# A meter of VectorE's backlog for the taps of a depthwise convolution, and tiles that rest behind their stores, in a four-layer vision kernel

## The chip, the core and the metric

The kernel runs on one core of a Trainium2 chip (trn2). The metric is the device time of one launch in microseconds; several runs are made and the median counts. The core has five engines with queues of their own, each worked off in order: PE (TensorE, with its weight loads listed as PEld), DVE (VectorE), ACT (ScalarE), POOL (GpSimd) and SP (SyncE, which here issues nearly all DMAs).

## The reference, cut to what matters

The input x has 4 images of 384 channels and 48 x 48 points, all float32. Four layers follow each other, each `x = x + layer(groupnorm(x))`:

```python
# layer 0: a state-space block over the 2304 points of an image, 768 inner channels, 16 states
xin, z = split(xs @ in_proj_w.T);  xin = silu(conv4(xin))
h = exp(dt * A) * h + dt * B * x;  y = sum(h * C)      # a scan along the points
out = layernorm((y + xin * D) * silu(z) @ out_proj_w.T)
# layer 1: 1x1 product, filter in 8x8 Fourier patches, depthwise 3x3, gate, 1x1 product
t = depthwise3x3(irfft2(rfft2(patches(x @ w_in)) * fft_filter));  out = (gelu(t1) * t2) @ w_out
# layer 2: depthwise 11x11 convolution with kernels made of 4 points
# layer 3: 4 experts, each relu(x @ w1 + b1) @ w2 + b2, weighted by a two-best gate
```

Layer 0 is the longest: per image 5 chunks of 460 or 464 points, 6 groups of 128 channels, 16 states, so 4 x 5 x 96 = 1920 scans of one tile each.

## The kernel before, in words

**One loop over the scans sets the order.** `scans` walks over u = 0 to 1919, and each u is a slot. A slot has one scan on DVE (L966), one decay `da` on ACT (L942), the product `bu` for three slots later on POOL (L953), and the product with C, which is done on DVE (L986) in a fast slot and on POOL (L995) in a slow one. From the second image on two slots of four are slow; in the first image it is one of three. PE adds up the states by transposing into PSUM (L886), three to five slots later. B and C are rows broadcast to 128 partitions by SP's DMAs (L930), issued three to four slots ahead into 3 and 4 buffers.

**Everything else is fitted in by tasks.** A task is a generator that yields before each step with a kind: "act" steps run at the start of a slot, "pe", "dve" and "pool" steps in the middle, "late" steps behind the slot's product. A step that yields n times before it is issued stands at least n slots later; `wait(n)` does only that. A lane holds a queue of tasks and runs up to `width` of them at a time. Lanes come in a fixed order: `aux` (layer 0's own work: projections L749 to L768, steps L866, gates L1023, out projections L1037 to L1050, norm and residual L1091 to L1095), `start` (work done early in the first image), `one` (layers 1 to 3 of the image before, up to the scores of the experts) and `two` (the experts of an image, whose first task needs the last task of lane `one`). Layers 1 to 3 of image b are queued in `one` at slot 480 (b + 1) + 42.

**Two things hold a step back.** `Meter(2.3, 3.7)` stands for PE's backlog in us: each slot takes 2.3 off and puts 0.44 on for the transposes, and a "pe" step with a weight waits until its weight fits under 3.7 (lane `aux` is let through but counted). A `Ring` stands for the buffers of a tag: a step that needs a buffer waits until the one that it would reuse is marked done. "Done" is said when the last reader is issued, so what it guards is the order of issue and not the end of a DMA.

**Layer 1** (L1306 to L1457): six strips of 8 rows an image. `patches` makes the Fourier filter in PSUM (the sum L1366 is DVE's); `finish_strip` runs the depthwise 3x3: nine taps on DVE for each of three channel groups (`taps`, L1413 the first, L1415 the others), one PSUM accumulator for all (`accr`), a copy or GELU on ACT between groups, two products (L1430, L1437), then three products on PE (L1443, L1447) with a sum and statistics on DVE (L1452, L1454), and a store (L1457). `slow_slot()` gives the taps 3 places in a slow slot and 2 in a fast one.

**Layer 2** (L1491 to L1582): bands of 9 or 10 rows; `load_band` brings the band into `xb` (L1513), `windows` runs 8 matmuls for a block of 8 rows (L1557), and the last adds the sum into `xb` (L1578, L1580) and stores it (L1582). `xb` has two buffers. **Layer 3**: scores (L1649 to L1671), then `experts`: for each of 4 experts 16 blocks of 144 points; `load3` brings x (`xe`, L1737) and from the second expert on the running sum y (`ye`, L1740), two products follow on PE (L1750), the sum on DVE (L1782, or three L1785 for the first expert) and a store (L1791) of y, or of x with the sum in it for the first expert, and of the output for the last. Behind the last scan the lanes are worked off, image 3 goes through layers 1 to 3, and `all_experts` does its experts from one set of weights (L1850 to L1882).

Of the kernel before, what the change touches and what calls it, by code (L numbers as in the profile page):

```python
# [16 lines left out]
P = 128  # L17
# [25 lines left out]

class Ring:


    def __init__(self, make, n):
        self.make, self.n, self.read = make, n, []

    def free(self, k=1):  # L50
        return all(self.read[: max(0, len(self.read) + k - self.n)])
# [6 lines left out]
    def done(self, k):  # L58
        self.read[k] = True


class Meter:


    def __init__(self, each, limit):
        self.each, self.limit, self.value = each, limit, 0.0

    def slot(self, given):
        self.value = max(0.0, self.value - self.each) + given
# [25 lines left out]
class Lane:  # L95
# [7 lines left out]
    def step(self, phase, slot, at=0):  # L103
        for task in self.active:
            if task.ended:
                continue
            kind, weight, ring, when = task.next
            if PHASE.get(kind, 1) != phase or task.after > slot:
                continue
            if weight and self.bound and self.meter.value + weight > self.meter.limit:  # L110
                continue
            if (ring and not ring[0].free(ring[1])) or (when and not when()):
                continue
            self.meter.value += weight
            task.move(slot)
        self.active = [t for t in self.active if not t.ended]
        while (
            self.queue and len(self.active) < self.width and self.queue[0].at <= max(at, slot)
            and all(t.ended for t in self.queue[0].needs)
        ):  # L120
            task = self.queue.pop(0)
            task.move()
            if not task.ended:
                self.active.append(task)

    def drain(self, slot, others=()):
        n = 0
        while self.queue or self.active:
            self.meter.value = 0.0
            for phase in range(3):  # L130
                for lane in (self, *others):
                    lane.step(phase, slot + n, 1 << 30)
            n += 1
            assert n < 20000, "stuck"
# [8 lines left out]
def tile_layers(ctx: ExitStack, tc: tile.TileContext, a: dict, out: bass.AP):  # L143
# [22 lines left out]
    gexp = const("gexp", [GROUPS, C], a["c_gexp"])  # L166
# [8 lines left out]
    def group_norm(st, bank, mean, rstd, name):  # L175

        mv = small.tile([P, CT, 2], F32, name=f"mv{name}", tag="mv")
        for ct in range(CT):
            nc.vector.bn_aggr(mv[:, ct, :], st[:, ct].rearrange("p k s -> p (k s)"))

        def to_groups(src, n, what):
            ps = bank(f"g{what}{name}")
            for ct in range(CT):
                nc.tensor.matmul(
                    ps[:GROUPS, :n], lhsT=gsel[:, ct, :], rhs=src(ct),
                    start=ct == 0, stop=ct == CT - 1,
                )
            return ps[:GROUPS, :n]

        def to_channels(src, n, what):  # L190
            ps = bank(f"c{what}{name}")
            for ct in range(CT):
                nc.tensor.matmul(
                    ps[:, n * ct : n * ct + n], lhsT=gexp[:, bass.ts(ct, P)], rhs=src,
                    start=True, stop=True,
                )
            return ps[:, : n * CT]

        grp = small.tile([GROUPS, 2], F32, name=f"grp{name}", tag="grp")
        nc.vector.tensor_copy(grp, to_groups(lambda ct: mv[:, ct, :], 2, "m"))  # L200
        nc.vector.tensor_copy(mean, to_channels(grp[:, 0:1], 1, "m"))
        dev = small.tile([P, CT], F32, name=f"dev{name}", tag="dev")
        nc.vector.tensor_sub(dev, mv[:, :, 0], mean)
        nc.vector.tensor_mul(dev, dev, dev)
        var = small.tile([GROUPS, 1], F32, name=f"var{name}", tag="var")
        nc.vector.scalar_tensor_tensor(
            var, to_groups(lambda ct: dev[:, ct : ct + 1], 1, "v"), GN_EPS, grp[:, 1:2],
            ALU.add, ALU.add,
        )
        nc.gpsimd.tensor_tensor(var, var, neghalf[:GROUPS, 0:1], ALU.pow)  # L210
        nc.vector.tensor_copy(rstd, to_channels(var, 1, "v"))

    def group_norm_steps(st, ring, mean, rstd, name):
# [15 lines left out]
        def to_channels(src, n, what):  # L229
            ps, k = ring.take(f"c{what}{name}")  # L230
            for ct in range(CT):
                nc.tensor.matmul(
                    ps[:, n * ct : n * ct + n], lhsT=gexp[:, bass.ts(ct, P)], rhs=src,
                    start=True, stop=True,
                )
            return ps[:, : n * CT], k
# [179 lines left out]
    with ExitStack() as first:  # L416
# [55 lines left out]
        stats0 = wp.tile([P, 2, CT, 2, 3, 6], F32, name="stats0")  # L472
# [86 lines left out]
        def scans(wk, mm, ring, meter, place, lanes, begin):  # L559
# [9 lines left out]
            def image_stats(b, ct, h):  # L569
# [4 lines left out]
                for k in range(3):  # L574
                    yield ("dve",)
                    nc.vector.bn_stats(stats0[:, b % 2, ct, h, k, :], t[:, bass.ts(k, LB)])

            def image_norm(b):
                yield from group_norm_steps(
                    stats0[:, b % 2].rearrange("p c h k s -> p c (h k) s"), ring,  # L580
# [4 lines left out]
            def early_stats(b, ct, h):  # L585
# [6 lines left out]
                for k3 in range(3):  # L592
                    yield ("dve",)
                    nc.vector.bn_stats(st[:, ct, h, k3, :], t[:, bass.ts(k3, LB)])
# [8 lines left out]
            def early_fold(b):  # L603
# [21 lines left out]
                yield ("dve",)  # L625
# [11 lines left out]
            def early_z(b, t, j):  # L637
# [22 lines left out]
                yield ("pool",)  # L660
# [28 lines left out]
            def fold(b, which):  # L689
# [22 lines left out]
                yield ("dve",)  # L712
# [25 lines left out]
            def project(i, j):  # L738
# [27 lines left out]
                yield ("dve",)  # L766
# [74 lines left out]
            def steps(i, p):  # L841
# [22 lines left out]
                yield ("dve",)  # L864
# [146 lines left out]
            def gate(i, m):  # L1011
# [9 lines left out]
                yield ("late",)  # L1021
# [4 lines left out]
            def out_proj(i, k):  # L1026
# [20 lines left out]
                yield ("dve",)  # L1047
# [4 lines left out]
            def layer_norm(i):  # L1052
# [8 lines left out]
                yield ("dve",)  # L1061
# [12 lines left out]
            def residual(i, ct):  # L1074
# [14 lines left out]
                yield ("dve",)  # L1089
# [86 lines left out]
            for tag, shape, n in (  # L1176
# [7 lines left out]
                    n,  # L1184
# [14 lines left out]
            with tc.manual_schedule():  # L1199
# [10 lines left out]
                for u in range(N + 6):  # L1210
# [17 lines left out]
                    meter.slot(0.44)  # L1228
                    soon = u % PAIR >= 8
# [25 lines left out]
                while aux.queue or aux.active:  # L1255
                    at += 1
                    meter.slot(0.0)
                    for phase in range(3):
# [5 lines left out]

        def slow_slot():
            return place[0] % 4 < 2

        def later(b, ring, accr):
# [11 lines left out]
            def slots(tag, shape, n):  # L1280

                return Ring(
                    lambda name: d["wk"].tile(shape, F32, name=name, tag=tag, bufs=n), n
# [11 lines left out]
            def begin1():  # L1295
# [3 lines left out]
                w = d["w_out"] = wk.tile([P, 2, C], F32, name=f"w_out1_{b}", tag="w_out", bufs=1)  # L1299
                nc.sync.dma_start(w[:, 0, :], a["L1_w_outT"][:P, :])  # L1300
                nc.sync.dma_start(w[64:P, 1, :], a["L1_w_outT"][P:, :])
# [38 lines left out]
            def patches(hb, wb):  # L1340
# [24 lines left out]
                yield ("late",)  # L1365
# [27 lines left out]
            def finish_strip(hb):  # L1393
# [7 lines left out]
                def taps(ct):  # L1401
# [3 lines left out]
                    room = 3 if slow_slot() else 2  # L1405
                    for k in range(9):
                        if not room:
                            yield ("dve",)
                            room = 3 if slow_slot() else 2
                        room -= 1  # L1410
# [18 lines left out]
                yield ("dve",)  # L1429
# [6 lines left out]
                yield ("dve",)  # L1436
# [3 lines left out]
                for ct in range(CT):  # L1440
# [3 lines left out]
                        ps[:, :LB], lhsT=w[:, 0, bass.ts(ct, P)], rhs=act[:, 0, :],  # L1444
# [3 lines left out]
                        ps[:, :LB], lhsT=w[64:P, 1, bass.ts(ct, P)], rhs=act[64:P, 1, :],  # L1448
                        start=False, stop=True,
                    )  # L1450
                    yield ("late",)
# [26 lines left out]
            xbs = slots("xb", [P, max(BANDS) * W], 2)  # L1478
# [68 lines left out]
            def windows(ct, k, r, first, last, final):  # L1547
# [26 lines left out]
                if last:  # L1574
                    yield ("late",)
# [5 lines left out]
                    yield ("pool",)  # L1581
# [40 lines left out]
            xg = slots("xg", [P, CT, LB], 2)  # L1622

            def begin3():
# [16 lines left out]
                yield ("dve",)  # L1641
# [4 lines left out]
            def scores_of(hb):  # L1646
# [23 lines left out]
                yield ("dve",)  # L1670
# [17 lines left out]
        def experts(b, ring, rings):  # L1688
# [15 lines left out]
            def begin(e):  # L1704
# [21 lines left out]
                yield ("late",)  # L1726
# [4 lines left out]
            def load3(s, e):  # L1731
                yield (
                    "pool", 0, None,
                    lambda: rings["xe"].free() and (not e or rings["ye"].free()),
                )
                x = take(("x", s, e), "xe", f"xe{b}_{s}_{e}")
                nc.sync.dma_start(x, strip(x3d[b], bass.ts(s, EB)))  # L1737
                if e:
                    y = take(("y", s, e), "ye", f"ye{b}_{s}_{e}")
                    nc.sync.dma_start(y, strip(y3d, bass.ts(s, EB)))  # L1740
                yield from wait(3)

            def block(s, e):
# [33 lines left out]
                yield ("late",)  # L1777
                key = ("y" if e else "x", s, e)
                x = d[key][0]
                if e:  # L1780
                    y = x.rearrange("p c t -> p (c t)")
                    nc.vector.tensor_add(y, ps[:, : CT * EB], y)  # L1782
                else:
                    for m in range(CT):
                        nc.vector.scalar_tensor_tensor(  # L1785
                            x[:, m, :], ps[:, bass.ts(m, EB)], b2_sum[:, m : m + 1],
                            x[:, m, :], ALU.add, ALU.add,
                        )
                ring.done(r)
                yield ("pool",)  # L1790
                nc.sync.dma_start(strip(out[b] if e == NE - 1 else y3d, bass.ts(s, EB)), x)  # L1791
                done(key)
# [106 lines left out]
        def of_experts(pool, sizes):  # L1899
            for tag, n in sizes.items():  # L1900
# [5 lines left out]
                    n,  # L1906
# [11 lines left out]
        meter = Meter(2.3, 3.7)  # L1918
        one, two = Lane(8, meter), Lane(4, meter)

        def begin(b):
# [10 lines left out]
            {"we": 1, "xe": 2, "ye": 2, "hr": 1},  # L1932
        )
        with (
# [7 lines left out]
            while not all(ring.read):  # L1942
# [6 lines left out]
        with (  # L1949
# [4 lines left out]
            of_experts(wk, {"we": 2, "xe": 3, "ye": 3, "hr": 3})  # L1954

            one.queue += later(NB - 1, ring, accr)
            while one.queue or one.active or two.queue or two.active:
                at += 1
                meter.slot(0.0)
                if not (one.queue or one.active):  # L1960
# [124 lines left out]
```

## Time and profile before

| | |
|---|---|
| median of 3 runs | 5400.23 us (5399.6 to 5402.55) |
| the profiled execution | 5405.14 us |
| its span, first to last instruction | 5403.1 us, mean granted TensorE clock 0.919 |
| busy: PE, PEld, DVE, ACT, POOL | 4646.1, 3666.7, 4067.1, 2989.0, 3363.1 us |
| first and last scan start | 86.5 and 4515.3 us |
| taps (L1415) | 576, 348.0 us in all, 615 ns each |
| SP's DMAs | 787.38 MB of 794.36 MB in all |

Busy times are sums over the whole span; stages with different limits lie in them, so the profile is read by stretches. A wait names the engine that stood, the line that it stood at, what released it, the total in us, how often, and the longest.

### The profile page before, as it was taken

Reading aid. Unit: us, or ns where it says so; the run is one execution under the profiler, and the core shown is the slowest. Engines: PE = TensorE matmul, PEld = TensorE weight load, DVE = VectorE, ACT = ScalarE, POOL = GpSimd, SP = SyncE. Lnnn points to the kernel's source line nnn. Section 1 sums busy time; section 2 is a strip of 40 time slices with the busy share of each in tenths; the row PEclk is TensorE's granted clock in tenths of the full one; section 3 lists DMA queues with packets and bytes.
Section 4 is the critical chain, followed back from the end, with each engine's and each line's share of the span. In section 5 each row is a group of like instructions: output and inputs, shape, how many; then the busy total and the mean of one; then the engine's idle time right before and its main releaser. Section 6 shows DMA issues by size and latency. Waiting matters only on the chain. (4 is left out here: it accounts for less than half of the span.)

```text
span 5403.1 us, 82006 instructions
## 1 busy us (share of the span) xinstructions
PE 4646.1 (86%) x27796; PEld 3666.7 (68%) x27796; DVE 4067.1 (75%) x5581; ACT 2989.0 (55%) x6632; POOL 3363.1 (62%) x3020
## 2 busy tenths in 40 slices
PE   5898877787768988888889988888799988999899
PEld 3555545454446766765668867665678877889799
DVE  5998899889997888889887778798987875452200
ACT  3566655565547765565567745565477653335321
POOL 3788778886677788876678678775677783000000
PEclk8898987788879999998899999998899999999899
DMA  4565545443344555655566565655566573543210
GB/s 152 172 187 175 178 128 150 129 143 120 111 127 131 148 165 157 191 161 147 149 172 178 161 200 155 173 146 149 154 182 174 158 213 115 175 138 105 64 27 23
DMA packets 648873, 794.36 MB, mean 147 GB/s; under 512 B 60149, under 2 KB 642661, under 8 KB 648062
## 3 DMA queue, kind: packets, MB, share of 16 engines
q1 hardware_dynamic: 638148, 787.38, 49.9%
q8 instruction: 221, 3.62, 0.3%
q10 hardware_dynamic: 10298, 1.67, 0.2%
q14 instruction: 206, 1.69, 0.1%
HBM read 685.04 MB, written 103.81 MB: 146 GB/s over the span
## 5 line engine op out<-in xcount | busy, mean ns | idle before, releaser
L953 POOL TENSOR_TENSOR bu<-u,B 128x460 f32<-128x460 f32 (+1 forms) x1920 | 2227.0, 1170 | 795.5 <-DVE g L966 349.8
L942 ACT ACTIVATE da<-dt,a_neg 128x460 f32<-128x460 f32 (+1 forms) x1920 | 1242.4, 648 | 310.6 <-DVE g L986 185.6
L886 PE MATMUL y<-ident,g 128*115 128x128 f32 (+1 forms) x7680 | 1111.3, 292 | 192.5 <-DVE g L986 114.8
L886 PEld LDWEIGHTS y<-ident,g 128*115 128x115 f32 (+1 forms) x7680 | 991.2, 183 | 400.4 <-DVE g L986 140.5
L995 POOL TENSOR_TENSOR g<-g,C 128x460 f32<-128x460 f32 (+1 forms) x885 | 1030.0, 1164 | 246.8 <-ACT carry L980 244.3
L966 DVE TENSOR_TENSOR_SCAN da<-da,carry,bu 128x460 f32<-128x460 f32 (+1 forms) x828 | 971.7, 1174 | 122.2 <-ACT da L942 76.7
L966 DVE TENSOR_TENSOR_SCAN g<-da,carry,bu 128x460 f32<-128x460 f32 (+1 forms) x708 | 819.8, 1167 | 57.7 <-issue 18.8
L986 DVE TENSOR_TENSOR g<-da,C 128x460 f32<-128x460 f32 (+1 forms) x1035 | 656.4, 634 | 175.7 <-DMA C<-bcd 62.0
L980 ACT COPY carry<-da 128x1 f32<-128x1 f32 x828 | 130.3, 157 | 760.5 <-DVE g L986 758.0
L1750 PE MATMUL pout<-hr,we 128*128 128x144 f32 x3456 | 485.0, 297 | 51.5 <-ACT hr L1766 37.8
L1750 PE MATMUL ph<-xe,we 128*128 128x144 f32 x3456 | 484.7, 298 | 33.6 <-DMA xe<-x3d 18.9
L1750 PEld LDWEIGHTS pout<-hr,we 128*128 128x128 f32 x3456 | 456.3, 197 | 75.3 <-ACT hr L1766 47.9
L1750 PEld LDWEIGHTS ph<-xe,we 128*128 128x128 f32 x3456 | 459.4, 199 | 51.5 <-DMA xe<-x3d 13.7
L1557 PE MATMUL pc<-band,row 128*128 128x162 f32 (+14 forms) x3456 | 451.3, 284 | 11.2 <-ACT row L1544 10.9
L1557 PEld LDWEIGHTS pc<-band,row 128*128 128x128 f32 x3456 | 440.0, 194 | 16.6 <-ACT row L1544 11.9
L749 PE MATMUL pin<-xch,w_inx 128*128 128x463 f32 (+2 forms) x720 | 344.8, 621 | 55.1 <-DMA xch<-in_x 32.3
L1415 DVE SCALAR_TENSOR_TENSOR dw<-pad,w_dw,dw 128x384 f32<-128x384 f32 x576 | 348.0, 615 | 20.4 <-ACT pad L1390 9.6
L1037 PE MATMUL po<-w_out,zs 128*115 128x384 f32 (+1 forms) x960 | 342.2, 499 | 14.7 <-DVE ye L1782 9.3
L1766 ACT ACTIVATE hr<-ph,nb 128x144 f32<-128x144 f32 x576 | 176.2, 376 | 279.2 <-PE ph L1750 278.4
L1524 ACT ACTIVATE rep<-x,br,wr 128x192 f32<-128x192 f32 x576 | 273.7, 540 | 4.2 <-issue 4.2
L768 DVE SCALAR_TENSOR_TENSOR xc<-pin,conv_w,xc 128x460 f32<-128x460 f32 (+1 forms) x360 | 249.2, 692 | 30.7 <-ACT xc L762 18.5
L749 PEld LDWEIGHTS pin<-xch,w_inx 128*128 128x128 f32 x720 | 143.8, 213 | 179.8 <-issue 136.3
(211 smaller groups left out, 5979.2 us busy)
## 6 DMA issues: line engine op xcount, KB each, us to landing
B<-bcd SPq DMA_DIRECT2D x768, 230.0 KB, 3.6
C<-bcd SPq DMA_DIRECT2D x768, 230.0 KB, 4.0
B<-bcd SPq DMA_DIRECT2D x192, 232.0 KB, 3.8
C<-bcd SPq DMA_DIRECT2D x192, 232.0 KB, 4.3
xe<-x3d SPq DMA_DIRECT2D x192, 216.0 KB, 2.8
ye<-y3d SPq DMA_DIRECT2D x144, 216.0 KB, 2.8
y3d<-ye SPq DMA_DIRECT2D x96, 216.0 KB, 2.2
xs<-x1d SPq DMA_DIRECT2D x24, 576.0 KB, 5.2
```

What stands on the lines that cost most here:

```text
L749: nc.tensor.matmul(ps[:, lo : halo + n], lhsT=w_inx[:, k, bass.ts(j, P)], rhs=c["x"][:, k, lo : halo + n], start=k == 0, stop=k == CT - 1,)
L886: nc.tensor.matmul(c["y", m][:w, bass.ts(k, P)], lhsT=src[:, bass.ts(k, w)], rhs=ident, is_transpose=True, start=c["terms", m] == 1 and k ...
L942: nc.scalar.activation(da[:, :n], c["dt", p][:, m % 2, :n], AF.Exp, scale=a_neg[:, m, s : s + 1])
L953: nc.gpsimd.tensor_mul(bu[:, :n], c["u", p][:, m % 2, :n], live["B", u // 2][:, :n])
L966: nc.vector.tensor_tensor_scan(here[:, :n], da[:, :n], bu[:, :n], last if t else nil[:, 0:1], ALU.mult, ALU.add,)
L986: nc.vector.tensor_mul(live["g", u][:, :n], live["h", u][:, :n], live["C", u // 2][:, :n])
L995: nc.gpsimd.tensor_mul(g[:, :n], g[:, :n], live["C", u // 2][:, :n])
L1037: nc.tensor.matmul(ps[:w, :C], lhsT=c["zs"][:, m, bass.ts(k, w)], rhs=w_out0[:, m, :], start=m == 0, stop=m == MT - 1,)
L1415: nc.vector.scalar_tensor_tensor(v, src, w_dw[:, ct, k : k + 1], v, ALU.mult, ALU.add)
L1524: nc.scalar.activation(rep[:, :, n, :, :].rearrange("p g r c -> p r g c"), rows.rearrange("p (r g c) -> p r g c", r=BR, c=BC), AF.Identity ...
L1557: nc.tensor.matmul(d["acc2"][0][:, : BANDS[k] * W].rearrange("p (h w) -> p h w", w=W)[:, lo - edges[k] : hi - edges[k], xlo:xhi], lhsT=d[" ...
L1750: nc.tensor.matmul(ps[:, bass.ts(m, EB)], lhsT=w[:, k, bass.ts(m, P)], rhs=of[:, k, :], start=k == 0, stop=k == CT - 1,)
```

## The change

The taps are let in by a second meter that counts DVE's work. `Meter` gets a lower bound and a test; "dve" and "late" steps carry weights in us that are added to `meter.vector`; each slot takes 2.4 off, not below -1.2, and puts on 1.17 (slow) or 1.74 (fast), or nothing behind the last scan. Only `taps` asks the meter before it goes on. The weights, which the diff below leaves out: image statistics 0.46, folds 0.2 and 0.3, a projection 2.0, the steps of two channel groups 1.1, a gate 0.54, an out projection 0.7, norm 0.1, residual 1.2; in layer 1 a tap 0.57, a filter 0.47, the products 0.56 and 0.45, a sum with statistics 1.05; the sum of a band 1.25; scores 0.3 and 0.9; an expert's bias 0.1 and its sum 0.52 (the first expert's 0.85).

A ring can have a rest: a buffer is free for reuse only that many slots after it was marked done. Rests: 2 for the first image's early tiles, `xb` and `ye`, 1 for `xg` and `xe`. Stores of early z, of `xb` and of the experts go from one slot of wait to two; `load3` waits two slots instead of three. `xb` has four buffers instead of two, `ye` three instead of two. The first expert's sum goes to `ye` instead of in place into `xe`. The store of layer 0's residual (L1095) and the load of its chunk (L731) stay where they are.

To make room, `stats0` has one buffer instead of two, and the second half of layer 1's `w_out` lies once and for all in unused partitions of `gexp`.

```diff
+CLOCK = [0]
 class Ring:
+    def __init__(self, make, n, rest=0):
+        self.make, self.n, self.read, self.rest = make, n, [], rest
     def free(self, k=1):
-        return all(self.read[: max(0, len(self.read) + k - self.n)])
+        return all(
+            v is not False and v + self.rest <= CLOCK[0]
+            for v in self.read[: max(0, len(self.read) + k - self.n)]
+        )
     def done(self, k):
-        self.read[k] = True
+        self.read[k] = CLOCK[0]
 class Meter:
+    def __init__(self, each, limit, least=0.0):
+        self.each, self.limit, self.least, self.value = each, limit, least, 0.0
     def slot(self, given):
-        self.value = max(0.0, self.value - self.each) + given
+        self.value = max(self.least, self.value - self.each) + given
+    def admits(self, weight):
+        return self.value + weight <= self.limit
...
     def step(self, phase, slot, at=0):
+        CLOCK[0] = slot
...
-            if weight and self.bound and self.meter.value + weight > self.meter.limit:
+            meter = self.meter if kind == "pe" else self.meter.vector
+            if kind == "pe" and weight and self.bound and not meter.admits(weight):
                 continue
...
-            self.meter.value += weight
+            meter.value += weight
...
-    gexp = const("gexp", [GROUPS, C], a["c_gexp"])
+    gexp = cp.tile([P, C], F32, name="gexp")
+    nc.sync.dma_start(gexp[:GROUPS, :], a["c_gexp"])
+    nc.scalar.dma_start(gexp[64:P, :], a["L1_w_outT"][P:, :])
...
-        stats0 = wp.tile([P, 2, CT, 2, 3, 6], F32, name="stats0")
+        stats0 = wp.tile([P, 1, CT, 2, 3, 6], F32, name="stats0")
...
                 ring.done(r)
-                yield ("pool",)
+                yield from wait(2)
                 nc.sync.dma_start(zd[b][bass.ts(j, P), bass.ds(starts[t], n)], z[:, :n])
...
                     meter.slot(0.44)
+                    meter.vector.slot(0.0 if u >= N else 1.17 if where(u)[4] else 1.74)
...
-        def slow_slot():
-            return place[0] % 4 < 2
...
-                    room = 3 if slow_slot() else 2
                     for k in range(9):
-                        if not room:
+                        while not meter.vector.admits(0.57):
                             yield ("dve",)
-                            room = 3 if slow_slot() else 2
-                        room -= 1
+                        meter.vector.value += 0.57
...
-                        ps[:, :LB], lhsT=w[64:P, 1, bass.ts(ct, P)], rhs=act[64:P, 1, :],
+                        ps[:, :LB], lhsT=gexp[64:P, bass.ts(ct, P)], rhs=act[64:P, 1, :],
...
-            xbs = slots("xb", [P, max(BANDS) * W], 2)
+            xbs = slots("xb", [P, max(BANDS) * W], 4, 2)
...
                     nc.vector.bn_stats(stats3[b % 2][:, ct, k, :], x[:, :n])
-                    yield ("pool",)
+                    yield from wait(2)
                     nc.sync.dma_start(x3d[b][of_band(ct, k)], x[:, :n])
...
-            xg = slots("xg", [P, CT, LB], 2)
+            xg = slots("xg", [P, CT, LB], 2, 1)
...
-                    lambda: rings["xe"].free() and (not e or rings["ye"].free()),
+                    lambda: rings["xe"].free() and rings["ye"].free(),
...
-                yield from wait(3)
+                yield from wait(2)
...
-                            x[:, m, :], ps[:, bass.ts(m, EB)], b2_sum[:, m : m + 1],
+                            y[:, m, :], ps[:, bass.ts(m, EB)], b2_sum[:, m : m + 1],
                             x[:, m, :], ALU.add, ALU.add,
                         )
+                    done(("x", s, e))
                 ring.done(r)
-                yield ("pool",)
-                nc.sync.dma_start(strip(out[b] if e == NE - 1 else y3d, bass.ts(s, EB)), x)
-                done(key)
+                yield from wait(2)
+                nc.sync.dma_start(strip(out[b] if e == NE - 1 else y3d, bass.ts(s, EB)), y)
+                done(("y", s, e))
...
         meter = Meter(2.3, 3.7)
+        meter.vector = Meter(2.4, 3.4, -1.2)
...
-            {"we": 1, "xe": 2, "ye": 2, "hr": 1},
+            {"we": 1, "xe": 2, "ye": 3, "hr": 1}, {"xe": 1, "ye": 2},
```

## The prediction

> **What bounds the kernel now.** One core, span 5403.1 us in an execution of 5405.1 (2.0 us lie around the span), 4.9 over the median of 5400.2; my sum is made on 5405.1 and its difference carried to the median. I call each of the 1920 scan steps a slot. First I read the table of stretches, cut where layers change: its columns are stretch, length, busy us and count of PE, PEld, DVE, ACT, POOL, then granted clock, DMA share, GB/s.
>
> ```profile
> core 0: us, PE busy (x) PEld busy (x) DVE busy (x) ACT busy (x) POOL busy (x), PEclk, DMA share, GB/s
> 1240.00:1626.00 386.00, 278.46 (x1134) 175.82 (x1134) 355.63 (x503) 200.90 (x439) 264.37 (x239) 0.81 0.38 117
> 1626.00:1961.00 335.00, 303.35 (x1990) 250.99 (x1990) 265.19 (x322) 255.21 (x584) 255.82 (x228) 0.94 0.49 141
> 1961.00:2354.00 393.00, 347.12 (x2100) 268.07 (x2101) 334.36 (x453) 229.41 (x470) 327.09 (x295) 0.96 0.59 173
> 2354.00:2721.00 367.00, 302.32 (x1620) 226.61 (x1620) 337.36 (x484) 197.25 (x450) 238.30 (x215) 0.90 0.51 150
> 2721.00:3105.00 384.00, 362.25 (x2599) 316.04 (x2598) 304.06 (x385) 282.11 (x663) 280.14 (x250) 0.98 0.60 173
> 3105.00:3548.00 443.00, 386.12 (x2448) 311.18 (x2448) 356.83 (x477) 241.37 (x510) 343.72 (x310) 0.94 0.61 175
> ...
> 4516.00:4925.00 409.00, 385.61 (x2580) 334.29 (x2580) 176.00 (x350) 121.03 (x294) 3.73 (x13) 0.97 0.49 141
> ```
>
> Row 4 is layer 1 of image 1: DVE is busy 0.92, PE 0.82. Row 5 is its layer 2: PE 0.94. Row 6 is expert work: PE 0.87, DVE 0.81, so neither is full. The row at 4516 follows the last scan: PE 0.94. The same table for the scan line alone counts the slots:
>
> ```profile
> 1240.00:1626.00 386.00, 170.57 (x147) 0.81 0.38 117
> ...
> 2354.00:2721.00 367.00, 152.53 (x131) 0.90 0.51 150
> ...
> 3105.00:3548.00 443.00, 220.63 (x191) 0.94 0.61 175
> ...
> 4297.00:4516.00 219.00, 119.29 (x104) 0.95 0.67 193
> ```
>
> A slot of layer 1 costs 367/131 = 2.80 us (image 0: 386/147 = 2.63; image 2: 366/131 = 2.79), one of expert work 443/191 = 2.32, at the end 219/104 = 2.11. The groups of instructions give the taps:
>
> ```profile
> L1415 DVE SCALAR_TENSOR_TENSOR dw<-pad,w_dw,dw 128x384 f32<-128x384 f32 x576 | 348.0, 615 | 20.4 <-ACT pad L1390 9.6
> ```
>
> Is DVE full in layer 1? Layer 0 asks per slot 1.17 (scan) + half of 0.634 (product, L986), and per 96 slots 18 x 0.692 + 6 x 0.625 + 6 x 0.623 + 4 x 0.725 + 0.6 + 3 x 1.261 = 27.2: 1.771 in all. Layer 1 per image: 144 taps x 0.615 + 18 x 0.603 + 18 filters x 0.548 + 12 products x 0.55 + 18 x 1.109 = 136 us, 129 of it inside the stretch (six filters, three sums and a product fall outside). 131 x 1.771 + 129 + 17 expert adds x 0.6 = 371, against 367: DVE is full, and durations overlap by 1%.
>
> Then the SP queue. Its waits (us, times, longest) name stores that wait for their result, and loads that wait for the store from the same tile:
>
> ```profile
> SPq L1740 <- DMA y3d<-ye: 244.6, 92, 7.5
> SPq L1791 <- DVE ye L1782: 240.2, 91, 7.6
> SPq L1737 <- DMA y3d<-xe: 156.8, 47, 8.0
> SPq L1513 <- DMA x3d<-xb: 139.0, 52, 5.6
> ```
>
> With L1582 behind xb (116.4), L1740 behind out (113.9), L661 (104.3) and L1791 behind xe (82.0) that is 1197 us. The timeline shows what stands behind: the store leaves at 2840.24, the next load of xb stands until 2845.40, and B and C of the scan behind it:
>
> ```profile
> 2840.24 0.32 SPq L1582 DMA_DIRECT2D x3d<-xb  x1
> 2845.40 0.32 SPq L1513 DMA_DIRECT2D xb<-x2d  x1
> 2845.82 0.38 SPq L930 DMA_DIRECT2D B<-bcd  x1
> ```
>
> What the engines lose by it, from the waits (POOL's bu for B: 98.2 in 49 waits):
>
> ```profile
> DVE g L986 <- DMA C<-bcd: 62.0, 28, 6.1
> ```
>
> **The taps' meter.** Before, 2 or 3 taps enter per slot whatever else DVE has. After, a tap enters only while the backlog plus 0.57 is within 3.4; 2.4 drains per slot, not below -1.2. In the diff's own weights: layer 0 puts in (1.17 + 1.74)/2 + 25/96 (six projections at 2.0, three steps at 1.1, six gates at 0.54, four times 0.7, three times 1.2, and 0.1) = 1.715 per slot, experts about 0.11 (a block of 0.52 per 4.7 slots). 0.575 is left; without experts 0.685. A strip weighs 27 x 0.57 + 3 x 0.47 + 0.56 + 0.45 + 3 x 1.05 = 20.96, six weigh 125.8. The store of credit is 3.4 + 1.2 = 4.6. So layer 1 needs at least (125.8 - 4.6)/0.575 = 211 slots, 80 more than now; image 0, which has no experts beside it, 177 instead of about 138. That is arithmetic of the weights, not an estimate of speed.
>
> What does a slot then cost? 211 x 1.771 + 129 + 42 x 0.6 = 528, over 211 and less 1%: 2.48 at a full DVE. PE has 302/131 = 2.31 per slot, 0.93 of that. Bounds: 2.48, and 2.31/0.872 = 2.65 if PE again reaches only row 6's share. I take 2.53, 2% above DVE's own need, because the nearest row (layer 1 now) runs at DVE's need; for image 0, (177 x 1.771 + 129)/177 less 1% = 2.47, taken as 2.50.
> - Image 0: 177 x 2.50 = 442, for 138 x 2.63 = 363 and 39 displaced slots at 393/183 = 2.15 (84): -5.
> - Image 1: 211 x 2.53 = 534, for 367 and 80 displaced slots at 2.32 (186): -19. Experts of image 0 are nearly done when layer 2 starts, so its 134 slots fall from 384/158 = 2.43 towards 335/144 = 2.33: -13. Some 44 slots then hold no expert work (image 1's wait for its scores), 2.15 for 2.32: -7.
> - Image 2: 534 for 366 and 80 displaced slots at 2.11 (169): -1; layer 2, by half: -6.
>
> The scans gain 51.
>
> **What is late next.** Counted by the scans that started before them, the scores of an image now end 106 slots ahead of the next image's start (1376 against 1482), so 80 fit. Those of image 2 end at slot 1856; 80 later is past 1920. The 18 first-expert adds before 4516, six blocks, move behind the last scan: 6 x 18 matmuls x 0.287 = 31 us on a PE that is 0.94 busy there. The scores follow too: image 3 takes 27 from its last band (5056) to its last score (5083). Together +58.
>
> **Rings at rest, stores one step later.** A load asks for its tile one or two slots after the store was issued, and a store leaves a slot (2.3 us) after its result was put in DVE's order; L1791 waits 2.6 us on average now. Behind SP's wait stand B and C; behind those POOL and DVE. Of SP's waits these 1197 are 75%; some 390 (xch, xr, x2d, bcd, x2, xg) stay. So C's direct loss falls by 0.75 x 62, and of B's 98 little reaches the scan, which idles only 34.8 for bu. Zero if PE hides it, at most 62 + 35 + 33 (PE's own waits for xe) = 130. I take 35: C's row, half or so hidden where PE is 0.94 busy. Behind the scans xe and ye cost 12 + 9 + 8 of waits; I take -8.
>
> The third ye and a load that waits 2 slots instead of 3 also let blocks follow faster: bounds 0 and rows 3 and 6 and the stretch 4297 to 4516 (PE 192.6 of 219) brought from 0.87 or 0.88 to 0.94 of PE (25 + 34 + 15, half of it where layer 1 displaces them: 40). I take 0, as experts now wait for scores rather than tiles, and keep 40 for a rival. The e = 0 block writes ye instead of xe: the same three adds. Early z takes one slot more per tile, in image 0: its last is at slot 289 of 480. Free: w_out's half (one 96 KB load at the start instead of four), stats0 single.
>
> [...] A credit of 4.6 lets eight taps in at once, 4.9 us of DVE, before the scan that PE waits for. [...] By the row, layer 1 already keeps PE idle for 18% of the time and still has a clock of 0.90. And nine slots between strips drain 5.2 while 5.0 comes in, so there is no credit to burst with. I take 0.
>
> **Sum.** -51 + 58 - 35 - 8 = -36: 5405.1 becomes 5369, the median 5364.
>
> **Rivals.**
> - Slower: PE and DVE hamper each other in the longer layer 1, whose slot costs 2.65. 599 slots x 0.12 = +72: 5436. It decides from 2.59, where 36/599 = 0.06 is used up. For it: row 6, with neither engine full. Against: row 4, where DVE runs at its need with PE at 0.82. Chance 0.27.
> - No gain: SP's waits were hidden by PE. Without 35, 5399. For: PE 0.94 in row 5. Against: DVE's own 62. Chance 0.13, for all that ends within 0.2% (11 us, what a measurement here can tell).
> - More: experts fill the slots that layer 1 leaves, -40 besides: 5324. For: PE 0.87 in row 6. Against: they must wait for scores. Chance 0.20.
> - That the meter binds nothing and layer 1 keeps its 131 slots: excluded by 211.
>
> The likeliest, 0.40, is 5364, in 5340 to 5389. Range 5295 to 5440. Faster 0.60, same 0.13, slower 0.27.
>
> **What would show it.** Taps of an image over about 211 slots at about 2.53; PE clock there above 0.90; SP's L1513, L1737 and L1740 waits nearly gone, B's and C's down by two thirds; image 2's scores after the last scan; the time behind it near 938 us, not 888. Wrong if the slot stays at 2.65 or above, or if SP waits go and PE's share in expert work doesn't rise.

## The result, and the profile after

The changed kernel takes 5331.75 us (5328.5 to 5337.28), 5399.91 before beside it: a ratio of 0.9877, 95% interval 0.986 to 0.9894, 68 us less where 36 were forecast. The profiled execution has a span of 5327.4 us, 75.7 less than before. First the table of stretches of the kernel after: layer 1 of image 0, layer 1 of image 1, its layer 2, and the time behind the last scan. Columns as before: stretch, length, busy us and count of PE, PEld, DVE, ACT, POOL, then clock, DMA share, GB/s.

```profile
1226.00:1672.00 446.00, 315.69 (x1340) 201.72 (x1338) 412.21 (x570) 245.82 (x531) 323.24 (x291) 0.83 0.41 119
2339.00:2851.00 512.00, 441.28 (x2726) 357.62 (x2724) 472.82 (x664) 297.68 (x696) 370.79 (x332) 0.95 0.60 176
2851.00:3260.00 409.00, 391.98 (x2762) 340.12 (x2763) 328.27 (x415) 287.36 (x624) 307.68 (x272) 0.97 0.59 167
...
4424.00:4910.00 486.00, 478.69 (x3366) 418.89 (x3365) 189.78 (x386) 179.21 (x433) 3.73 (x13) 1.00 0.49 143
```

Row 2 against 2354 to 2721 before: DVE is as full as it was (0.92), but PE is at 0.86 instead of 0.82 and its clock is 0.95 instead of 0.90. The last row is PE at 0.985, where 4516 to 4925 before had 0.943. The scans alone, in the same stretches and for image 2:

```profile
1226.00:1672.00 446.00, 209.04 (x180) 0.83 0.41 119
...
2339.00:2851.00 512.00, 239.41 (x206) 0.95 0.60 176
...
3480.00:3987.00 507.00, 235.62 (x203) 0.94 0.58 169
```

So layer 1 takes 180, 206 and 203 slots at 2.48, 2.49 and 2.50 us. SP's waits, after:

```profile
SPq L1802 <- DVE ye L1792: 136.2, 66, 7.1
...
SPq L1748 <- DVE ye L1795: 119.6, 29, 27.0
SPq L1748 <- PE ph L1761: 113.3, 58, 8.7
...
SPq L1751 <- DMA y3d<-ye: 75.1, 42, 6.4
...
SPq L1524 <- DMA x3d<-xb: 16.8, 9, 3.3
```

And what the engines lose by them, POOL for B before, then POOL for B and DVE for C after:

```profile
POOL bu L953 <- DMA B<-bcd: 98.2, 49, 7.2
```

```profile
POOL bu L968 <- DMA B<-bcd: 17.4, 15, 2.1
...
DVE g L1001 <- DMA C<-bcd: 2.8, 3, 1.5
```

The load of a band stood 139 us behind its store and now stands 17; the load of y 245, now 75; that of x behind the first expert's store 157, now none, but it stands for the readers of its tile instead (120 and 113). B costs POOL 17 instead of 98 and C costs DVE 3 instead of 62.

### The profile page after: what moved, and what is told of

It reads as the page before. It is cut to its first block, busy times and chain, and to the rows that moved or that the text cites. A ratio compares the mean times of both kernels' runs of the same rounds, so it can differ in the third digit from the quotient of the medians.

```text
span 5327.4 us, 81986 instructions
## 1 busy us (share of the span) xinstructions
PE 4596.3 (86%) x27796; PEld 3643.1 (68%) x27796; DVE 4053.4 (76%) x5581; ACT 2987.0 (56%) x6632; POOL 3362.8 (63%) x3020
## 5 line engine op out<-in xcount | busy, mean ns | idle before, releaser
L1761 PE MATMUL ph<-xe,we 128*128 128x144 f32 x3456 | 473.2, 293 | 29.4 <-DMA xe<-x3d 6.1
L764 PE MATMUL pin<-xch,w_inx 128*128 128x463 f32 (+2 forms) x720 | 319.7, 583 | 20.0 <-DMA xch<-in_x 8.8
L981 DVE TENSOR_TENSOR_SCAN da<-da,nil,bu 128x460 f32<-128x460 f32 x207 | 242.5, 1171 | 32.1 <-ACT carry L995 26.6
```

What stands on the lines that cost most here:

```text
L764: nc.tensor.matmul(ps[:, lo : halo + n], lhsT=w_inx[:, k, bass.ts(j, P)], rhs=c["x"][:, k, lo : halo + n], start=k == 0, stop=k == CT - 1,)
L981: nc.vector.tensor_tensor_scan(here[:, :n], da[:, :n], bu[:, :n], last if t else nil[:, 0:1], ALU.mult, ALU.add,)
L1761: nc.tensor.matmul(ps[:, bass.ts(m, EB)], lhsT=w[:, k, bass.ts(m, P)], rhs=of[:, k, :], start=k == 0, stop=k == CT - 1,)
```

## Where the time went

Start times of the scans cut the span at the same slots in every kernel. Lengths in us; the last column is from the last scan to the end, and the blocks are those of image 2's first expert that are done before it (16 less a third of its sums behind the last scan). The executions profiled for rings_alone and meter_alone were 8 and 7 us above the medians of these kernels.

| kernel | 0 to 566 | 566 to 1047 | 1047 to 1527 | 1527 to 1919 | behind | blocks |
|---|---|---|---|---|---|---|
| before | 1136.5 | 1132.4 | 1193.8 | 966.0 | 887.9 | 6 |
| after | 1140.2 | 1115.5 | 1140.9 | 938.0 | 905.5 | 0 |
| after_again | 1145.3 | 1121.2 | 1141.3 | 935.8 | 901.5 | 0 |
| rings_alone | 1143.5 | 1133.6 | 1182.4 | 961.8 | 843.9 | 12 |
| meter_alone | 1140.5 | 1122.2 | 1173.4 | 939.1 | 909.5 | 0 |

The blocks can be counted by the experts' second products behind the last scan. A block has 18 of them and 18 first products, and image 2 has 64 blocks. Before, after and rings_alone:

```profile
L1750 PE MATMUL pout<-hr,we 128*128 128x144 f32 x1044 | 142.9, 292 | 7.9 <-ACT hr L1766 7.6
```

```profile
L1761 PE MATMUL pout<-hr,we 128*128 128x144 f32 x1152 | 155.1, 289 | 6.9 <-ACT hr L1777 6.7
```

```profile
L1766 PE MATMUL pout<-hr,we 128*128 128x144 f32 x936 | 126.8, 289 | 6.9 <-ACT hr L1782 6.6
```

So 58, 64 and 52 blocks were left at the last scan. The 18 second products take 155.1/64 = 2.42 us of PE, since they overlap, and the 18 first ones as much (155.0 in all, in after_again): a block costs 4.85 us.

## The experiments

My theory: layer 1 gets cheaper per slot, is paid for by later scores and experts, and the rings free SP. Rivals: the rings do it all; or bursts matter and not how thin the taps lie. The kernel before took 5409 us beside the first eight of these runs, 5410 beside the next three and 5403 beside the last.

**rings_alone**: the changed kernel with the old rule in `taps`.

```diff
+                    room = 3 if slow_slot() else 2
...
-                        while not meter.vector.admits(0.57):
+                        if not room:
                             yield ("dve",)
-                        meter.vector.value += 0.57
+                            room = 3 if slow_slot() else 2
+                        room -= 1
```

> The changed kernel with the old rule for the taps (3 in a slow slot, 2 in a fast one) and all rings, rests and later stores of the change. If the thinner layer 1 gives part of the gain (my theory): layer 1 back to about 131 slots at 2.8 us, SP waits as low as in the changed kernel, time near 5355, that is 43 of the 68 us. If the rings give it all and the meter's gain is given back later: 5332.

5347.3 us, 0.9887 (0.9872 to 0.9901): 62 us less than before, between the two. Layer 1 is back at 131 slots and 2.79 us; B and C cost 18 and 5. The rings alone give more than the 43 I counted, and they give it behind the last scan (888 to 844): six more blocks of experts are done before it.

**meter_alone**: the meter, with rests at 0, two buffers of xb and ye, one slot before a store, three before a load's products, and the first expert in place.

```diff
-            v is not False and v + self.rest <= CLOCK[0]
+            v is not False
...
-                yield from wait(2)
+                yield ("pool",)
...
-            {"we": 1, "xe": 2, "ye": 3, "hr": 1}, {"xe": 1, "ye": 2},
+            {"we": 1, "xe": 2, "ye": 2, "hr": 1}, {"xe": 1, "ye": 2},
```

> The taps' meter with the old rings, stores and in-place first expert of the kernel before. My theory: taps over 200 to 211 slots at 2.5 us, SP's waits as before, time near 5375. If the meter's gain is given back by later scores and a longer tail: 5395 to 5400. If the meter gives everything: 5332.

5367.1 us, 0.9925 (0.9912 to 0.9937): 42 us less. Taps over 180, 199 and 202 slots at 2.49 to 2.52; SP's wait of y behind its store stays at 218 us. Both parts alone are worth 104 together, and 74 in one kernel (next run): they don't add up.

**after_again**: no edit.

> The changed kernel once more, on the chip and beside the runs of the others. Both parts together should again give 0.9877 of the time before. If it is nearer 0.9887 than that, the meter adds nothing measurable to the rings.

5334.7 us, 0.9863 (0.9848 to 0.9878). On top of the rings the meter gives 13 us; the intervals of the two overlap a little. The table says how so little comes of it: after_again gains 12, 41 and 26 on rings_alone before the last scan and loses 58 behind it, 12 blocks of 4.85 us.

**meter_22** and **meter_27**: the drain per slot, `Meter(2.2, 3.4, -1.2)` and `Meter(2.7, 3.4, -1.2)`.

> The changed kernel with a drain of 2.2 a slot instead of 2.4. By the same arithmetic layer 1 needs (125.8 - 4.6)/(2.2 - 1.715 - 0.11) = 323 slots, so image 1's scores come after the next image's start at slot 1482 and image 2 doesn't reach its layer 2 before the last scan. My theory (the price of thinning is paid in later starts): slower than the changed kernel by 60 to 150 us, with a tail of over 1000 us. If DVE's evenness alone counts: 5332 or less.

> The changed kernel with a drain of 2.7 a slot: layer 1 needs 121.2/0.875 = 139 slots, about what the old rule takes. My theory: a slot of layer 1 at about 2.75 and the time of rings_alone, near 5350. If the bursts that the meter forbids are what matters, and not how thin the taps lie: 5332.

2.2: 5393.6 us, 0.9967 (0.9954 to 0.998), 59 more than the changed kernel: layer 1 of image 1 took 304 slots, its scores ended at slot 1568, and 1071 us lie behind the last scan. The theory had said 60 to 150 more. 2.7: 5372.2 us, 0.9932 (0.992 to 0.9944), where I expected 5350. Layer 1 took 132, 150 and 150 slots at 2.75, 2.66 and 2.70; scores of image 2 come 25 slots later than in rings_alone, four blocks are done before the last scan instead of 12. That covers the loss behind the last scan; image 0's stretch (slots 566 to 1047) is 12 us longer too, for which no run gives the cause. Of the three drains 2.4 is the best.

**old_taps_image2**: the changed kernel with the old rule for image 2 alone.

```diff
+                    room = 3 if slow_slot() else 2
...
-                        while not meter.vector.admits(0.57):
+                        if b != 2:
+                            while not meter.vector.admits(0.57):
+                                yield ("dve",)
+                        elif not room:
                             yield ("dve",)
+                            room = 3 if slow_slot() else 2
+                        room -= 1
```

> The changed kernel with the old rule of 3 and 2 taps for image 2 only. Stretch by stretch, rings_alone is 37 us faster than the changed kernel from slot 1527 on, and 60 us slower before. If stretches add up: 37 us less than the changed kernel, 0.981. If what counts is how much expert work is left at the last scan (lane two starts image 1's experts at slot 1479 either way): within 10 us of the changed kernel, since expert work only moves.

5375.4 us, 0.9938 (0.9924 to 0.9951): 41 more than the changed kernel, where one theory said 37 less and the other no change. Both fell. The rows from image 2's first tap (slot 1527) on. First after_again: about the first 131 slots of layer 1, the other 72, the rest of the scans, the time behind, and all four together:

```profile
3491.00:3815.00 324.00, 285.71 (x1675) 224.24 (x1674) 298.00 (x431) 189.53 (x442) 233.04 (x210) 0.95 0.56 161
3815.00:3998.00 183.00, 155.97 (x989) 129.94 (x988) 170.79 (x235) 104.18 (x243) 133.56 (x120) 0.93 0.62 183
3998.00:4428.00 430.00, 402.55 (x2982) 358.92 (x2980) 345.46 (x435) 293.47 (x643) 333.00 (x296) 0.98 0.61 178
4428.00:5333.00 905.00, 871.07 (x6428) 797.79 (x6428) 238.62 (x527) 293.43 (x747) 8.70 (x18) 0.98 0.32 94
3491.00:5333.00 1842.00, 1715.30 (x12071) 1510.88 (x12069) 1052.87 (x1624) 880.61 (x2074) 708.30 (x641) 0.97 0.46 134
```

Then this kernel: the 131 slots of its layer 1, the rest of the scans, the time behind, and all:

```profile
3490.00:3866.00 376.00, 307.72 (x1613) 232.79 (x1611) 339.77 (x502) 197.14 (x446) 238.40 (x214) 0.88 0.48 140
3866.00:4472.00 606.00, 571.69 (x4064) 497.25 (x4064) 481.82 (x604) 392.21 (x887) 464.42 (x413) 0.96 0.63 185
4472.00:5377.00 905.00, 865.39 (x6392) 800.61 (x6392) 235.05 (x519) 289.67 (x742) 5.26 (x15) 0.97 0.31 91
3490.00:5377.00 1887.00, 1744.80 (x12069) 1530.64 (x12067) 1056.64 (x1623) 879.02 (x2073) 708.08 (x640) 0.95 0.45 131
```

So thin taps are worth 45 us for one image (1887 against 1842), with the same work behind slot 1527 to two of 12070 matmuls. DVE is full in both layers 1: from scan to scan the durations of its instructions add up to 366 us of 375 here and to 505 of 503 in after_again. A slot costs 376/131 = 2.87 here and 507/203 = 2.50 there. The longer layer 1 takes 131 us more and holds 72 slots more, which here cost 606/261 = 2.32 each behind it (167); the 189 slots left cost 9 less. That is the price by slots of the prediction, and it makes the 45.

PE's own time for these matmuls is 30 us longer here, and 22 of the 30 lie in the first 131 slots, at a clock of 0.88 against 0.95. The trace shows the clock as either full or half: half for some 90 us there (0.88 over 376 us) against some 35 (0.95 over 324). But those are the slots in which DVE is full and PE busy 0.82, so the slower clock isn't shown to cost time. Nor did all other work stay where it was: this kernel does image 2's scores, 17 us of PE, before the last scan and a block of image 1's experts behind it, after_again the other way round. rings_alone was faster from there on because it had done experts earlier, not because of its taps.

**experts_old** undoes the experts' part (ye of two, in place, no rest, three slots for a load, one for a store); **rest_zero** sets all rests to 0 and keeps the rest of the change.

> The changed kernel with the experts' part undone: ye of two buffers, the first expert in place in xe, no rest for both, three slots of wait for a load, one for a store. The meter, and the rests of xb, xg and early z, stay. If the stores and loads of the experts are what the rings free (838 of the 1197 us of SP's waits): waits of POOL and DVE for B and C back to over 80 us, and about 0.9915, near the meter alone (0.9925). If the bands count for most: 0.988.

> The changed kernel with every rest at 0; the later stores, the third ye, four xb and the first expert's way stay. If the rest is what frees SP (the loads that stand behind a store, 655 of the 1197 us): those waits come back and the ratio is about 0.990. If the additional buffers do it, so that the tile that a load gets has long been stored: SP's waits stay low and 0.988.

experts_old: 5362.3 us, 0.9906 (0.9891 to 0.9921), 28 us of the change's 74; B and C cost 65 and 31 again. rest_zero: 5366.2 us, 0.9921 (0.9908 to 0.9935), 31 us; B and C cost 36 and 21. Its SP waits:

```profile
SPq L1748 <- PE ph L1761: 242.5, 77, 10.3
SPq L1751 <- DMA y3d<-ye: 198.6, 71, 6.7
```

For the experts the additional buffer doesn't do it by itself: without the rest a load is issued as soon as its tile may be named, and stands in SP's queue. For the bands it does: their load waits 11 us here, with four buffers and no rest, and 12 in experts_old. So of the rings' parts the rest of the experts' tiles is the likeliest to count: both runs take it away and lose about as much. Neither takes it away alone, as rest_zero takes the rests of `xg` and of the early tiles too.

**floor_0**: `Meter(2.4, 3.4, 0.0)`. **drain_image0**: in `begin1` of layer 1,

```diff
+                meter.vector.each = 2.2 if b == 0 else 2.4
```

> The changed kernel with the meter's lower bound at 0 instead of -1.2, so that at most six taps can enter at once and not eight. My reckoning is that a strip's pause drains 5.2 and puts in 5.0, so that no credit is left to burst with: same taps per slot and 0.986 again, within 5 us of the changed kernel. If bursts cost PE its clock: faster by 10 us or more, with a clock above 0.96 in layer 1 of images 1 and 2.

> The changed kernel with a drain of 2.2 for image 0 alone, 2.4 for the others. Lane two stands empty from slot 1408 to 1479, as image 1's scores come after image 0's experts, so experts of image 0 may start later at no price: slots 566 to 1047 fall by the 32 us that meter_22 shows there, image 0's experts end near slot 1445, and some of the moved expert work is paid in slots 1047 to 1479 (up to 18 us): 14 us less than the changed kernel, 0.984. If later experts are paid in full: no gain.

floor_0: 5321.1 us, 0.9843 (0.9826 to 0.986). Layer 1 took 194, 219 and 212 slots instead of 180, 206 and 203, so the credit below 0 had been used, against my reckoning. Clock 0.95 and 0.94 in layer 1 of images 1 and 2, as without it: bursts were not what it paid for. What it gains lies in slots 566 to 1047 (1103 instead of 1121) and, 10 us of it, before slot 566. No tap has run by then and PE's instructions have the same order in both, so these 10 aren't the edit's; without them little of the 14 is left. drain_image0: 5317.5 us, 0.9831 (0.9814 to 0.9848), 17 less than the changed kernel, 14 expected; 5 of the 17 lie before slot 566 here too. Slots 566 to 1047 fell by 40, the next stretch rose by 22, image 0's experts ended at slot 1444.

**more_rest**: the chunk's load waits two slots, its projections one more, and xe rests 2.

```diff
+                if i:
+                    yield from wait(2)
...
+                if i:
+                    yield from wait(1)
...
-{"xe": 1, "ye": 2},
+{"xe": 2, "ye": 2},
```

> The changed kernel with the chunk's load two slots later (and one slot more before its projections), so that it doesn't stand behind the residual's store, and a rest of 2 instead of 1 for xe. SP's waits of the chunk's load (70 us) and of xe behind the first expert's sums (95 us before the last scan) should go. If such waits still stand before B and C: 5 to 10 us less, 0.985. If what is left of them is covered (B and C cost 14 and 5 us now): the same within 5 us.

5367.5 us, 0.9929 (0.9911 to 0.9946): 33 more. SP stands at the chunk's load for 13 us instead of 70, but PE now stands for its data:

```profile
PE pin L766 <- DMA xch<-in_x: 39.8, 11, 6.3
```

That was 9.5 in after_again. 25 of the 33 us are lost before slot 1047, and experts start only at slot 983, so nearly all of these are the load's: PE stands 28 us for the chunk before slot 1047, 8 in after_again. For the other 8 the two edits aren't told apart, and the rest of xe has no price of its own.

**image0_and_floor**: the last two gains in one.

> The changed kernel with both: the drain of 2.2 for image 0 alone and a lower bound of 0. If the two add up (13 and 17 us less than the changed kernel): near 0.981. If both do the same thing, which is to thin image 0's layer 1 while lane two has no experts: the better of the two, 0.983, and image 0's experts end so late that image 1's must wait for them.

5323.7 us, 0.985 (0.9837 to 0.9864): they don't add up. Image 0's experts end at slot 1489, behind image 1's scores (1484), as the second case said. Of the kernels tried drain_image0 and floor_0 are the fastest, both faster than the kernels before and after by their medians; the interval of drain_image0 only touches that of the changed kernel, and the two aren't told apart.

## Why the prediction was right, and which terms were mis-sized

**Slots of layer 1: right.** 177, 211 and 211 were worked out of the weights; 180, 206 and 203 came, and 304 for a drain of 2.2 where 323 were expected. That the meter binds nothing was rightly excluded.

**Price of a slot: 2.50 and 2.53 forecast, 2.48 to 2.50 measured.** DVE's own need was 2.47 and 2.48; the 1 to 2% on top was for PE to hamper it, and PE didn't. The forecast had carried PE's 302/131 = 2.31 per slot over to the longer layer, though layer 1's own products then lie in 75 slots more; it measured 441/206 = 2.14. Over 180, 206 and 203 slots the price makes 4 + 9 + 7 = 20 us. The slower rival rested on 2.65 and fell with it.

**The scans: -51 forecast, -53 in meter_alone.** The sum is so near by luck. By stretch it is 10, 20 and 27 less (and 4 more before any tap) against 5, 39 and 7. Image 2's displaced slots were priced at 2.11, the price at the very end; the slots behind its layer 1 cost 2.30 on average, before (601/261) and after (434/189).

**The clock: 0 taken, no loss measured.** That eight taps at once could hold PE up at the price of its clock was a risk that I weighed and left out of the sum. No run shows such a cost: in layer 1 of image 1 the clock is 0.95 where it was 0.90, with PE busy 0.86 instead of 0.82, and old_taps_image2 has 0.88 against 0.95 in the same slots, with PE busy 0.82 against 0.88. What sets the clock no run shows. Whether the better clock gave any of the gain isn't shown. Over the whole span PE's busy time for the same 27796 matmuls was 4646.1 us before, 4642.4 in rings_alone and 4639.7 in meter_alone. The changed kernel has less, 4596.3 and 4609.2 (after_again), but meter_22, with the thinnest taps of all, has 4658.1. And "there is no credit to burst with" was wrong: floor_0 shows that the credit was used, though it isn't seen to have cost time.

**Behind the last scan: +50 forecast, +18 measured.** The six blocks moved as said. Their 31 was reckoned from 18 products a block at a whole length of 0.287; a block has 36, which overlap, so that two errors cancel: 6 x 4.85 = 29. The scores came behind the last scan too, but their 27 weren't paid: they ended at 4443, 21 us after the last scan began, beside layer 0's last chunk. And "I take -8" was too little: PE's busy time there rose by 35, from 836 to 871, but its idle time fell from 51 to 34.

**Rings: -43 forecast, -62 alone.** C's and B's waits went by more than two thirds, as named. SP's went less far than "nearly gone": the bands' did, y's fell from 245 to 75, and that of x became one for the readers of its tile. In the scans of rings_alone only 7 us show, with six more blocks (29 us of PE) done in them; the rest shows behind. The term that failed is "I take 0, as experts now wait for scores rather than tiles": with the old taps the experts do run faster, six blocks more before the last scan, which I had kept for the rival at 5324. In the changed kernel those blocks are the ones that the meter's late scores hold back again.

So the sum of -36 came from parts whose signs were right, with the experts' pace put too low and the time behind the scans too long. And the parts share one store, the expert work left at the last scan, so that 62 and 42 make 74.

What stays open: how much of PE's shorter time before slot 1527 is the clock and how much is work that moved, since no run fixes the work there; which of the rests and later stores counts for how much; and the price of the single `stats0` and of the new place of `w_out`, which stand in every run of the change.

## What to carry to other kernels

A burst of work on one engine that fills a stage is worth spreading only as far as nothing that comes behind it is the last to end: count the slots that it then takes from its own weights, and ask which chain starts later. In a queue that serves several streams in order, hold a load back until its tile's last store has had time to land. More buffers alone can free the queue, as four did for the bands (11 us of waits in rest_zero, 139 before), or not, as three for the experts (199, 245 before); and a load held back a slot too long is paid on the engine that waits for its data (PE stood 39.8 us for the chunk in more_rest, 9.5 in after_again). Measure such changes together and apart, since two that draw on the same slack don't add up.

## What the runs showed of the hardware

PE's busy time isn't a fixed sum: from slot 1527 on nearly the same matmuls (12071 and 12069) took 1715 us in after_again and 1745 in old_taps_image2, at mean clocks of 0.97 and 0.95; the edit between the two is how another engine's work is spread. Busy times of PE are to be compared with the clocks beside them. DVE ran layer 1 at its own need (2.49 against 2.48 us a slot) with PE busy 0.86 beside it, where I had expected some loss; its busy share reads 0.92 there, though the durations of its instructions fill the whole time (505 us of 503 for image 2, after_again).
